# A four-layer graph attention stack: the next batch's first norm emitted inside the last layer of the batch in front, with the ends of the program rearranged

## The chip, the cores and the metric

The kernel runs on one core of one Trainium2 chip. The metric is the device time of one execution in microseconds (us); lower is better. The engines are named as in the profile: PE is the matmul engine, PEld its weight load, DVE the vector engine, ACT the scalar engine, POOL is GpSimd, and SP issues most of the DMA transfers.

## The reference, cut to what matters

The input is `x`, 32 batches of 512 nodes with 256 features, and one 512 x 512 matrix `adj` for all batches. Four graph attention layers follow each other; every one adds its result to `x`, and every one starts with a norm over the features:

```python
h = jnp.maximum(_layernorm(x, axis=-1), 0.0)
x = x + _L0_gnn_ref(h, adj, L0_gnn_W, L0_gnn_a)   # mask adj, elu
h = jnp.maximum(_layernorm(x, axis=-1), 0.0)
x = x + _L1_gnn_ref(h, adj, L1_gnn_W, L1_gnn_a)   # mask adj, relu
h = jnp.maximum(_layernorm(x, axis=-1), 0.0)
x = x + _L2_gnn_ref(h, adj, L2_gnn_W, L2_gnn_a)   # four heads of 64, mask adj, elu
h = jnp.maximum(_layernorm(x, axis=-1), 0.0)
x = x + _L3_gnn_ref(h, adj, ...)                  # two attentions between two dense layers
```

In layers 0 to 2 the attention between nodes i and j is the softmax over j of `leaky_relu(s_i + s_j)`, where `s_i` and `s_j` are the products of node i's and node j's values with the two halves of a vector `a`, and only the pairs that `adj` allows count. Layer 3 is

```python
out = relu(x @ mlp1_w + mlp1_b);          residual = out
out = elu(gat(out, None, W_fc, a_fc)) + residual       # no mask, 512 features
out = relu(out @ mlp2_w + mlp2_b);        residual = out
out = elu(gat(out, adj, W_hand, a_hand)) + residual    # mask adj
return relu(out)
```

The kernel has a fast form, which holds for some kinds of input only, and a general form, which is there for all others. A flag that the fast form computes tells whether its result may be used. All that follows is about the fast form.

## The kernel before, in words

**Tiling.** A batch's 512 nodes are four tiles of 128 rows; its `x` is one SBUF tile, 128 x (4 x 256), which all four layers update in place. A layer takes the norm of the rows on DVE and ACT (`norm`: statistics at L268 and L269, the inverse deviation with a logarithm and an exponential at L271 and L272, the scaled rows `xn` at L275 or L279), transposes `xn` on PE (`turn_pair`, recorded at L70, with `hT` written by ACT at L289), multiplies by the layer's weights (`values`, PE at L66; its results `v` are written at L318 and L319 in layer 0 and at L321, L323 and L324 in layer 1), forms the unnormalised attention weights (`weights`, L352, on DVE), and multiplies these with `v` on PE (`averages`; a column of ones gives the row sums, of which L386 takes the reciprocal). `note` keeps the largest exponential for the flag.

**Two kinds of norm.** With `late=True` (L275) only the mean is subtracted, and the scale `rs` is applied after the product. With `late=False` (L279) DVE waits for the inverse deviation and applies both. The first norm of a batch and the norm at the end of layer 2, whose rows layer 3 takes, are of this second kind.

**Streams.** Stream i (0 to 3) works on the batches i, i+4, i+8 and so on; `NS` is 4. Each stream is a Python generator that emits instructions and then yields the time at which it would like to go on (`after_us(n)`, from a count of its own PE cycles and a pause). The loop at the end of `fast` always continues the stream with the smallest time. This makes an order of emission in which the four streams, at different layers, are interleaved; a scheduler then arranges the instructions within each engine, apart from the few that `keep_in_program_order` ties. Each stream owns two of the eight PSUM banks.

`batch(b)` is one batch of a stream. It takes the `x` that was loaded earlier, makes the first norm, and runs the layers:

```python
        xn, rs = new_xn(), small([NT], "rs")
        for t0 in range(0, NT, 2):
            norm(xt, xn, rs, t0, False)
        yield after_us(4)
```

The load of batch b+4 is issued after layer 2 of batch b. All streams share three buffers for `xn`.

**Layer 3.** The attention without mask has no need of a full 512 x 512 matrix: the nodes are sorted by one of the two sums (`sort_attend`: POOL scatters the rows at L606, running sums go to a table in DRAM, POOL gathers one row per node at L654, and DVE combines its halves at L669). Only the last batch uses the full matrix (`attend`). After the dense layer `mlp2` (its result is `rT`) comes the masked attention, and the last loop of `layer3` finishes the batch by two pairs of tiles: exponential and Relu on ACT (L698, L699), a minimum, an exponential and a sum (`elu2_plus1`, L409 to L411), the residual, transposed from `rT` (L709), the last Relu (L710), the addition to `x` on POOL (L712) and the store of 256 KB (L713).

**Start.** SP issues the loads in the order of the text: x of batch 0, W0, the two halves of a0, `adj`, x of batches 1 to 3, and the other weights. `finish_w` multiplies each weight matrix with its vector `a` (`scale_a` at L110 and L111, `project` at L120 and L126), which gives three more columns. The generator `setup`, emitted between the streams, turns `adj` into the transposed mask (L209, L210, L219), then prepares the later layers' weights, and then checks `adj` for negative entries with one reduction over all of it (`differ`, L225). The reduction keeps its place in the emitted order. At the end of the program (L774 to L783) the numbers kept by `note` and `differ` are reduced to the flag.

Of the kernel before, what the change touches and what calls it, by code (L numbers as in the profile page):

```python
# [24 lines left out]
OP = mybir.AluOpType  # L25
AX = mybir.AxisListType

EPS = 1.0e-5
P = 128
# [6 lines left out]
def fast(ctx, tc, flag, x, adj, w0, a0, w1, a1, w2, a2, mlp1_w, mlp1_b, mlp2_w, mlp2_b,  # L36
         w_fc, a_fc, w_hand, a_hand, out):
    nc = tc.nc
    B, N, F = x.shape
    NT = N // P  # L40
# [5 lines left out]
    NS = 4  # L46
# [13 lines left out]
    def after_us(us):  # L60

        return begun[0] + STRETCH * spent[0] / CYCLES + SLOW * us
# [5 lines left out]
    def transpose(p, x, i, tied=False):  # L68
        spent[0] += 2 * P
        instruction = nc.tensor.transpose(p, x, i)  # L70
        if tied:
            tc.keep_in_program_order(instruction)
# [4 lines left out]
    def bank():  # L77

        own = [turn[0], *(i for i in range(NS) if i not in active and i != turn[0])]
        banks[0] += 1  # L80
        return psum.tile([P, N], FP, tag=f"b{own[banks[0] % len(own)]}", name="b", bufs=8 // NS)
# [11 lines left out]
    def load_x(b):  # L93
        t = work.tile([P, NT, F], FP, tag="x", name="x", bufs=NS + 1)
        nc.sync.dma_start(t, x[b].rearrange("(t p) f -> p t f", p=P))
        return t


    def fetch_a(a, name):
        ft = a.shape[0] // (2 * P)  # L100
        t = const.tile([P, ft, 3], FP, name=name)
        for s, c in ((0, 2), (1, 0)):
            nc.sync.dma_start(
                t[:, :, c:c + 1],
                a[s * ft * P:(s + 1) * ft * P, :].rearrange("(t p) o -> p t o", p=P),
            )
        return t

    def scale_a(t, alpha):
        nc.vector.tensor_scalar_mul(t[:, :, 1:2], t[:, :, 0:1], alpha - 1.0)  # L110
        nc.vector.tensor_scalar_mul(t[:, :, 2:3], t[:, :, 2:3], 1.0 - alpha)  # L111

    def project(dst, block, k, a_cols):

# [13 lines left out]
    def fetch_w(w, a, name):  # L128

        kt, cols = w.shape[0] // P, w.shape[1]  # L130
        t = const.tile([P, kt, cols + 3], FP, name=name)
        wr = w.rearrange("(k p) f -> p k f", p=P)
        for c in range(0, cols, F):
            nc.sync.dma_start(t[:, :, c + (3 if c else 0):c + (3 if c else 0) + F], wr[:, :, c:c + F])
        return t, fetch_a(a, name + "a")

    def finish_w(fetched, alpha):
        t, a_cols = fetched

        def block(k, f):  # L140
            c = f * P + (3 if f * P >= F else 0)
            return t[:, k, c:c + P]

        scale_a(a_cols, alpha)
        for k in range(t.shape[1]):
            project(t[:, k, F:F + 3], block, k, a_cols)
            yield


    xts = {0: load_x(0)}  # L150
    W0, _ = fetched0 = fetch_w(w0, a0, "W0")
    adj_sb = work.tile([P, NT, N], I32, tag="w", name="adj", bufs=4)
    nc.sync.dma_start(adj_sb, adj.rearrange("(t p) j -> p t j", p=P))
    for b in range(1, NS):
# [1 line left out]
    W1, _ = fetched1 = fetch_w(w1, a1, "W1")  # L156
# [6 lines left out]
    for h in range(NH):  # L163
        t, r = divmod(h * D, P)
# [8 lines left out]
    WFC, _ = fetched3 = fetch_w(w_fc, a_fc, "WFC")  # L173
    WM2 = const.tile([P, KH, F], FP, name="WM2")
    nc.sync.dma_start(WM2, mlp2_w.rearrange("(k p) f -> p k f", p=P))
    WHA, _ = fetched4 = fetch_w(w_hand, a_hand, "WHA")
# [23 lines left out]
    differ = const.tile([P, 2], FP, name="differ")  # L200
# [5 lines left out]
    def setup():  # L206

        own = work.tile([P, NT, N], FP, tag="w", name="own", bufs=4)
        nc.vector.tensor_scalar(own, adj_sb, 0.0, None, op0=OP.is_gt)  # L209
        nc.gpsimd.affine_select(  # L210
            out=own, in_=own, pattern=[[P, NT], [-1, N]], base=0, channel_multiplier=1,
            compare_op=OP.not_equal, fill=1.0,
        )
        for j in range(NT):
            turn[0] = NS - 1 - j % (NS - 1)
            p = bank()
            for t in range(NT):
                transpose(p[:, t * P:(t + 1) * P], own[:, t, j * P:(j + 1) * P], ident, j + t == 0)
            nc.scalar.copy(maskT[:, j, :], p)  # L219
        turn[0] = NS - 1  # L220
        yield
        yield from finish_w(fetched1, 0.01)


        tc.keep_in_program_order(nc.vector.tensor_reduce(differ[:, 0:1], adj_sb, AX.XY, OP.min))  # L225
        nc.vector.tensor_scalar(differ[:, 0:1], differ[:, 0:1], 0.0, None, op0=OP.is_lt)
        least = small([1], "rden")
        nc.vector.tensor_reduce(least, diag, AX.X, OP.min)
        nc.vector.tensor_scalar(differ[:, 1:2], least, 0.0, None, op0=OP.is_le)
        nc.vector.tensor_copy(W2[:, :, :, :D], raw2.rearrange("p k (h d) -> p k h d", d=D))  # L230
        nc.vector.tensor_scalar_mul(A2v[:, :, 1:2], A2v[:, :, 0:1], -0.8)
        nc.vector.tensor_scalar_mul(A2v[:, :, 2:3], A2v[:, :, 2:3], 0.8)
        for k in range(KF):
            project(W2[:, k, :, D:], lambda k, f: raw2[:, k, f * P:(f + 1) * P], k, A2)
            yield
        yield from finish_w(fetched3, 0.2)

        for tri, sign in ((before, 1), (after, -1)):
            nc.vector.memset(tri, 1.0)
            nc.gpsimd.affine_select(  # L240
                out=tri, in_=tri, pattern=[[sign, P]], base=0, channel_multiplier=-sign,
                compare_op=OP.is_gt, fill=0.0,
            )
        ties = work.tile([P, 2 * N - P], FP, tag="w", name="ties", bufs=4)
        nc.vector.memset(ties, TINY)
        nc.gpsimd.affine_select(
            out=ties, in_=ties, pattern=[[-1, 2 * N - P]], base=N - P, channel_multiplier=1,
            compare_op=OP.is_gt, fill=0.0,
        )
        nc.vector.tensor_copy(band, ties)  # L250
        yield
        yield from finish_w(fetched4, 0.2)
# [3 lines left out]
    def small(shape, name):  # L256
        return work.tile([P] + shape, FP, tag=name, name=name, bufs=2 * NS)
# [33 lines left out]
    def turned(xn, when):  # L291

        hT = work.tile([P, KF, N], FP, tag="hT", name="hT", bufs=3)
        turn_pair(xn, hT, 0)
        yield when
        turn_pair(xn, hT, 2)
        yield after_us(0.6)
        return hT
# [78 lines left out]
    def pair(tag="y"):  # L377
        return work.tile([P, 2, F], FP, tag=tag, name=tag, bufs=3)
# [10 lines left out]
    def plain(hT, w, rs=None):  # L389
        v = yield from values(hT, w, rs)  # L390
        wt = weights(lambda t: v[:, t, F + 2:F + 3], lambda j: v[:, j, F + 1:F + 2])
        note(v[:, :, F:])
        yield after_us(3.2)
        return v, wt
# [294 lines left out]
    def layer3(xt, xn, when, b):  # L689
        oT = yield from linear_t((yield from turned(xn, when)), WM1, b1, "oT", 2)  # L690
        yield from (attend if b >= B - 1 else sort_attend)(oT, b)
        rT = yield from linear_t(oT, WM2, b2, "rT", 2)
        v, wt = yield from plain(rT, WHA)
        for t0 in range(0, NT, 2):
            y, q = pair(), pair("q")
            for i in range(2):
                p, rd = averages(v, wt, t0 + i)
                nc.scalar.activation(q[:, i, :], p, AF.Exp, scale=rd)  # L698
                nc.scalar.activation(y[:, i, :], p, AF.Relu, scale=rd)  # L699
                yield after_us(0)  # L700
            elu2_plus1(y, q)
            p = bank()
            for i in range(2):
                for k in range(KF):
                    transpose(
                        p[:, (i * KF + k) * P:(i * KF + k + 1) * P], rT[:, k, (t0 + i) * P:(t0 + i + 1) * P], ident
                    )
            yf = y.rearrange("p a f -> p (a f)")
            nc.vector.scalar_tensor_tensor(yf, p, -1.0, yf, op0=OP.add, op1=OP.add)  # L709
            nc.scalar.activation(y, y, AF.Relu)  # L710
            xr = xt[:, t0:t0 + 2, :]
            nc.gpsimd.tensor_tensor(xr, xr, y, op=OP.add)  # L712
            nc.sync.dma_start(  # L713
                out[b, t0 * P:(t0 + 2) * P, :].rearrange("(t p) f -> p t f", p=P), xr
            )
            yield after_us(0)

    def mlp_in(oT, y, t):
# [7 lines left out]
            o, p.rearrange("p (f c) -> p f c", c=P), -1.0, o, op0=OP.add, op1=OP.add  # L726
        )

    def batch(b):
        xt = xts.pop(b)  # L730
        xn, rs = new_xn(), small([NT], "rs")
        for t0 in range(0, NT, 2):
            norm(xt, xn, rs, t0, False)
        yield after_us(4)
        when = after_us(2)
        for layer in (layer0, layer1, layer2):
            xn, rs, when = yield from layer(xt, xn, rs, when)
        if b + NS < B:
            xts[b + NS] = load_x(b + NS)
        yield from layer3(xt, xn, when, b)  # L740
# [13 lines left out]
    while ready:  # L754
        i = min(ready, key=ready.get)
# [23 lines left out]
    p = bank()  # L779
# [437 lines left out]
```

## The time and the profile before

| | |
|---|---|
| median of 3 runs | 2943.76 us (2943.12 to 2945.2) |
| profiled execution, its own time | 2945.59 us |
| span of that execution in the profile | 2943.9 us |
| mean granted clock of PE | 0.995 of full speed |
| busy share: PE, PEld, DVE, ACT, POOL | 97%, 79%, 76%, 52%, 17% |
| DMA, mean over the span | 92 GB/s |

The span runs from the first to the last thing that the profiler recorded; the execution's own time is 1.7 us longer. A busy share is an average over the whole span, in which the start, the long middle and the end lie together. PE and PEld overlap, so their times are not added. In lines of groups, waits and timeline a value is named as the program names it: `xn<-x,mv,rs` writes `xn` from `x`, `mv` and `rs`. `L66` and `L70` are the lines of the helpers that record every matmul and every transpose, so that they hold the work of all layers, and the operands tell these apart. In a timeline a line is a run of equal instructions: its start, the time from its first start to its last end, the engine, what it does, how many (`x4`), and in brackets how long the engine had been idle in front of it and what it waited for.

### The profile page before, as it was taken

To read this page: it belongs to the slowest core of one execution; us is meant where nothing else is said; L and a number is where in the kernel's file an instruction comes from. 1 tells how busy PE (TensorE), PEld (TensorE's weight loads), DVE (VectorE), ACT (ScalarE), POOL (GpSimd) and SP (SyncE) were. 2 spreads that over 40 slices of the span, in tenths; PEclk is the share of its full clock that TensorE was granted. 3 is DMA by queue.
4 is the path that set the end of the run, shared out by engine and by line. 5 is a ranking of instruction groups with operands and counts; after the bars stand their busy time and mean duration, and the time that the engine had idled before them with its cause. 6 is when DMAs were issued, how large, how long until landed. Compare 5 with 4: busy or idle time off the path is not lost.

```text
span 2943.9 us, 43065 instructions
## 1 busy us (share of the span) xinstructions
PE 2863.2 (97%) x15177; PEld 2326.1 (79%) x15177; DVE 2224.0 (76%) x5674; ACT 1537.4 (52%) x3918; POOL 501.3 (17%) x509
## 2 busy tenths in 40 slices
PE   7999999999999999999999999999999999999988
PEld 6777888877887877888878888778888788887766
DVE  4677877778877778878777878777777788787764
ACT  4444455554555554555554555545555555555544
POOL 0011112111122111122021121121221111221120
PEclk9999999999999999999999999999999999999999
DMA  3033223233223233233332232332232322332230
GB/s 94 19 101 99 87 83 116 92 96 99 90 87 105 95 98 98 83 102 98 98 101 90 86 107 93 96 99 89 87 116 89 99 95 81 101 112 77 96 106 23
DMA packets 193150, 270.89 MB, mean 92 GB/s; under 512 B 16992, under 2 KB 156062, under 8 KB 192928
## 3 DMA queue, kind: packets, MB, share of 16 engines
q1 hardware_dynamic: 163168, 169.76, 18.5%
q0 software_dynamic: 29760, 98.30, 10.1%
q8 instruction: 123, 2.02, 0.3%
q14 instruction: 99, 0.81, 0.1%
HBM read 152.62 MB, written 115.39 MB: 91 GB/s over the span
## 4 chain that ended last, share of the span: by engine, by line
PE 77%; DVE 13%; ACT 5%; DMA 3%; issue 1%; POOL 0%; SPq 0%; POOLq 0%; ACTq 0%; DVEq 0%
PE b L66 70%; PE b L70 7%; DVE st L268 3%; DVE xn L279 1%; DMA order<-v,at 1%; DVE xn L275 1%; DVE sums L640 1%; DVE w L352 1%; ACT v L324 1%; DMA sums<-order 1%; DVE sums L631 1%; ACT y L504 1%; DVE x L405 1%; ACT q L503 1%; DVE y L404 1%
## 5 line engine op out<-in xcount | busy, mean ns | idle before, releaser
L66 PE MATMUL b<-v,w 128*128 128x65 f32 (+1 forms) x7232 | 1222.4, 321 | 6.8 <-DVE w L352 6.7
L66 PEld LDWEIGHTS b<-v,w 128*128 128x128 f32 x7232 | 1053.6, 192 | 167.8 <-issue 64.2
L66 PE MATMUL b<-WFC,oT 128*128 128x256 f32 (+1 forms) x2048 | 496.3, 380 | 0.0
L66 PEld LDWEIGHTS b<-WFC,oT 128*128 128x128 f32 x2048 | 373.6, 189 | 48.7
L66 PE MATMUL b<-W,hT 128*128 128x259 f32 (+1 forms) x1536 | 382.0, 387 | 9.2 <-ACT hT L289 4.4
L352 DVE SCALAR_TENSOR_TENSOR w<-b,v,maskT 128x512 f32<-128x512 f32 x512 | 369.0, 743 | 4.9 <-PE b L70 3.6
L606 POOL DMA_INDIRECT order<-v,at x248 | 284.2, 1146 | 491.2 <-DVE oT L725 152.0
L66 PEld LDWEIGHTS b<-W,hT 128*128 128x128 f32 x1536 | 283.0, 190 | 58.9 <-ACT v L324 8.9
L352 DVE SCALAR_TENSOR_TENSOR w<-spread,v,maskT 128x512 f32<-128x512 f32 x384 | 269.3, 741 | 0.0
L386 DVE RECIPROCAL rden<-b 128x1 f32<-128x1 f32 (+1 forms) x516 | 78.7, 164 | 246.5 <-PE b L66 243.2
L712 POOL TENSOR_TENSOR x<-x,y 128x512 f32<-128x512 f32 x64 | 81.3, 1270 | 1074.9 <-ACT y L710 963.8
L66 PE MATMUL b<-hT,WM 128*128 128x512 f32 x512 | 248.6, 596 | 0.7 <-ACT hT L289 0.7
L654 POOL DMA_INDIRECT g<-table,at x124 | 120.9, 975 | 724.8 <-ACT y L674 385.3
L66 PE MATMUL b<-oT,WM 128*128 128x512 f32 x512 | 230.3, 592 | 0.0
L528 ACT ACTIVATE v<-b,ends 128x256 f32<-128x256 f32 x256 | 118.6, 466 | 176.7 <-PE b L66 172.4
L268 DVE BATCH_NORM_STATS2 st<-x 128x6 f32<-128x256 f32 x512 | 192.7, 408 | 5.1 <-DMA x<-in_x_dram 2.6
L289 ACT ACTIVATE hT<-b 128x512 f32<-128x512 f32 x256 | 147.0, 590 | 83.8 <-PE b L70 83.8
L338 ACT ACTIVATE oT<-b,bias 128x512 f32<-128x512 f32 x128 | 87.7, 685 | 193.2 <-PE b L66 193.2
L411 DVE TENSOR_TENSOR y<-q,y 128x512 f32<-128x512 f32 x192 | 132.5, 690 | 67.0 <-ACT q L410 66.5
L70 PE MATMUL b<-ident,xn 128*128 128x128 f32 x1024 | 152.7, 279 | 23.5 <-DVE xn L279 20.9
L66 PEld LDWEIGHTS b<-oT,WM 128*128 128x128 f32 x512 | 97.0, 190 | 95.1 <-issue 91.8
L70 PEld LDWEIGHTS b<-ident,xn 128*128 128x128 f32 x1024 | 121.9, 143 | 60.6 <-DVE xn L279 33.8
(142 smaller groups left out, 3738.3 us busy)
## 6 DMA issues: line engine op xcount, KB each, us to landing
table<-sums SPq DMA_DIRECT2D x62, 1032.0 KB
sums<-order SPq DMA_DIRECT2D x62, 516.0 KB
spread<-row SPq DMA_DIRECT2D x96, 256.0 KB
x<-in_x_dram SPq DMA_DIRECT2D x32, 512.0 KB
out_dram<-x SPq DMA_DIRECT2D x64, 256.0 KB
sums<-order SPq DMA_DIRECT2D x62, 129.0 KB
order<-v,at POOLq DMA_INDIRECT x248
g<-table,at POOLq DMA_INDIRECT x124
```

Source lines behind the costliest of these rows:

```text
L66: nc.tensor.matmul(p, w, x, **flags)
L70: instruction = nc.tensor.transpose(p, x, i)
L268: nc.vector.bn_stats(st[:, i, :], xt[:, t0 + i, :])
L289: nc.scalar.activation(hT[:, :, t0 * P:(t0 + 2) * P], p.rearrange("p (k n) -> p k n", k=KF), AF.Relu)
L338: nc.scalar.activation(o[:, f, :], p, AF.Relu, bias=bias[:, f:f + 1])
L352: w = nc.vector.scalar_tensor_tensor(wt[:, j, :], r, t_col(j), maskT[:, j, :], op0=OP.max, op1=OP.mult)
L386: nc.vector.reciprocal(r, den)
L411: nc.vector.tensor_tensor(r, q, r, op=OP.add)
L528: nc.scalar.activation(halves[c][:, t, :F], ps[:, :F], AF.Copy, scale=ends[:, t, 0:1])
L606: nc.gpsimd.indirect_dma_start(out=orders[c], out_offset=bass.IndirectOffsetOnAxis(ap=at[:, 0, t:t + 1], axis=0), in_=halves[c][:, t, :], ...
L654: nc.gpsimd.indirect_dma_start(out=g, out_offset=None, in_=table, in_offset=bass.IndirectOffsetOnAxis(ap=at[:, 1, t:t + 1], axis=0),)
L712: nc.gpsimd.tensor_tensor(xr, xr, y, op=OP.add)
```

## The change

There are five edits; no result is computed differently.

1. The first norm of batches 4 to 31 moves. A new function `first_norm(b)` holds it. For batches 0 to 3 it is called at the start of `batch(b)` as before. For a later batch b+4 it is called in `layer3` of batch b, in the last loop, after the first pair of tiles has been emitted with its store and before the second pair. The instructions are the same.
2. `scale_a` works on POOL, not on DVE.
3. The two loads of a0 are issued ahead of x of batch 0 and of W0.
4. The reduction over `adj` (`differ`, L225 before, L215 after) and the comparison behind it are emitted ahead of the transposes of the mask, behind the mask's two elementwise steps.
5. In the last batch the last loop of `layer3` takes one tile at a time. There the addition to `x` is on DVE, and four stores of 128 KB take the place of two of 256 KB. All other batches keep pairs.

```diff
     def scale_a(t, alpha):
-        nc.vector.tensor_scalar_mul(t[:, :, 1:2], t[:, :, 0:1], alpha - 1.0)
-        nc.vector.tensor_scalar_mul(t[:, :, 2:3], t[:, :, 2:3], 1.0 - alpha)
+        nc.gpsimd.tensor_scalar_mul(t[:, :, 1:2], t[:, :, 0:1], alpha - 1.0)
+        nc.gpsimd.tensor_scalar_mul(t[:, :, 2:3], t[:, :, 2:3], 1.0 - alpha)
...
-        return t, fetch_a(a, name + "a")
+        return t, fetch_a(a, name + "a") if len(a.shape) == 2 else a
...
+    a0_sb = fetch_a(a0, "W0a")
     xts = {0: load_x(0)}
-    W0, _ = fetched0 = fetch_w(w0, a0, "W0")
+    W0, _ = fetched0 = fetch_w(w0, a0_sb, "W0")
...
             compare_op=OP.not_equal, fill=1.0,
         )
+        tc.keep_in_program_order(nc.vector.tensor_reduce(differ[:, 0:1], adj_sb, AX.XY, OP.min))
+        nc.vector.tensor_scalar(differ[:, 0:1], differ[:, 0:1], 0.0, None, op0=OP.is_lt)
         for j in range(NT):
...
-        tc.keep_in_program_order(nc.vector.tensor_reduce(differ[:, 0:1], adj_sb, AX.XY, OP.min))
-        nc.vector.tensor_scalar(differ[:, 0:1], differ[:, 0:1], 0.0, None, op0=OP.is_lt)
         least = small([1], "rden")
...
-        for t0 in range(0, NT, 2):
-            y, q = pair(), pair("q")
-            for i in range(2):
+
+        n = 1 if b == B - 1 else 2
+        for t0 in range(0, NT, n):
+            y, q = pair()[:, :n, :], pair("q")[:, :n, :]
+            for i in range(n):
...
-            nc.vector.scalar_tensor_tensor(yf, p, -1.0, yf, op0=OP.add, op1=OP.add)
+            nc.vector.scalar_tensor_tensor(yf, p[:, :n * F], -1.0, yf, op0=OP.add, op1=OP.add)
             nc.scalar.activation(y, y, AF.Relu)
-            xr = xt[:, t0:t0 + 2, :]
-            nc.gpsimd.tensor_tensor(xr, xr, y, op=OP.add)
+            xr = xt[:, t0:t0 + n, :]
+            (nc.gpsimd if n == 2 else nc.vector).tensor_tensor(xr, xr, y, op=OP.add)
             nc.sync.dma_start(
-                out[b, t0 * P:(t0 + 2) * P, :].rearrange("(t p) f -> p t f", p=P), xr
-            )
+                out[b, t0 * P:(t0 + n) * P, :].rearrange("(t p) f -> p t f", p=P), xr
+            )
+            if t0 == 0 and b + NS < B:
+                first_norm(b + NS)
             yield after_us(0)
...
+    normed = {}
+
+    def first_norm(b):
+
         xt = xts.pop(b)
         xn, rs = new_xn(), small([NT], "rs")
         for t0 in range(0, NT, 2):
             norm(xt, xn, rs, t0, False)
-        yield after_us(4)
+        normed[b] = xt, xn, rs
+
+    def batch(b):
+        if b < NS:
+            first_norm(b)
+            yield after_us(4)
+        else:
+            yield after_us(4)
+        xt, xn, rs = normed.pop(b)
         when = after_us(2)
```

More of the change, by code (lines that the diff above doesn't have):

```diff
@@ L702, in layer3 @@
             p = bank()
-            for i in range(2):
+            for i in range(n):
                 for k in range(KF):
@@ L727, in mlp_in @@
         )
-    def batch(b):
+    normed = {}
+    def first_norm(b):
         xt = xts.pop(b)
```

## The prediction, before the result was known

> **What bounds the kernel now.** I read the page first, then the stages, then who waits for whom, then the timeline where the waits are. The page's busy row:
>
> ```profile
> PE 2863.2 (97%) x15177; PEld 2326.1 (79%) x15177; DVE 2224.0 (76%) x5674; ACT 1537.4 (52%) x3918; POOL 501.3 (17%) x509
> ```
>
> The same by stretches (length; busy us of PE, PEld, DVE, ACT, POOL; granted clock, DMA share, GB/s):
>
> ```profile
> 0.00:40.00 40.00, 28.30 (x138) 22.96 (x139) 16.20 (x56) 13.56 (x34) 4.08 (x10) 0.91 0.60 172
> 40.00:200.00 160.00, 147.67 (x804) 120.47 (x803) 107.93 (x310) 67.79 (x191) 11.65 (x12) 0.99 0.14 45
> 200.00:2700.00 2500.00, 2466.42 (x13144) 2009.12 (x13143) 1947.80 (x4958) 1337.70 (x3420) 445.68 (x448) 1.00 0.30 95
> 2700.00:2944.00 244.00, 220.82 (x1096) 173.60 (x1094) 152.06 (x352) 118.38 (x276) 39.90 (x39) 0.96 0.23 75
> ```
>
> PE is busy for 98.7% of the middle stretch; in all it idles 80.7 us, of which 33.6 lie there, 24.0 before 200 us and 23.2 after 2700. A change that leaves PE's work alone can win from these alone. The waits of PE (us in total, times, longest) say whom it waits for:
>
> ```profile
> PE b L70 <- DVE xn L279: 20.9, 33, 1.7
> PE b L70 <- ACT v L324: 13.0, 29, 0.9
> ```
>
> L279 is the norm's last step, with which two norms end: a batch's first, and that of its layer 3. Following the 256 L279 instructions in order tells them apart: 18.2 of the 20.9 us stand before the first transpose of a new batch. One such place (batch 19), PE alone and then DVE alone:
>
> ```profile
> 1620.90 1.91 PE L66 MATMUL b<-WFC,oT 128*128 128x259 f32 x8
> 1622.65 0.60 PE L70 MATMUL b<-ident,xn 128*128 128x128 f32 x4
> 1623.09 3.22 PE L66 MATMUL b<-WFC,oT 128*128 128x259 f32 x14
> 1627.11 0.77 PE L70 MATMUL b<-ident,xn 128*128 128x128 f32 x4 [0.80 <-DVE xn L279]
> 1627.71 0.60 PE L66 MATMUL b<-WFC,oT 128*128 128x259 f32 x2
> ```
> ```profile
> 1618.93 0.17 DVE L386 RECIPROCAL rden<-b 128x1 f32<-128x1 f32 x1 [3.28 <-PE b L66]
> ...
> 1626.64 1.51 DVE L279 TENSOR_SCALAR xn<-x,mv,rs 128x256 f32<-128x256 f32 x4
> 1628.07 0.75 DVE L669 SCALAR_TENSOR_TENSOR g<-g,ends 128x516 f32<-128x516 f32 x1
> ```
>
> The transposes stand in PE's queue before their norm is done, while DVE had idled 3.28 us eight us earlier. The real loss is over the 0.80 shown: eight WFC passes from 1620.90 to 1622.65 make 0.22 each, so the 14 from 1623.09 would have released PE at 1626.16, and it started at 1627.11 (0.95 lost); four transposes take 0.44 in flow (1622.65 to 1623.09) and took 0.60 here (0.16 lost). Together 1.11.
>
> **The skill.** "TensorE: Matmul & The Clock Gate", section "Part 1: The HAM clock gate", says that PE falls to half rate after an idle window. It does so here: the granted clock is 0.50 from 26 to 32 us after a 2.73 us wait, and the passes come every 0.43 us. "SBUF — State Buffer", section "SBUF: two separate sides", says that VectorE and GpSimd lock a shared port pair for a whole instruction; the last L409 below took 1.23 us beside POOL's L712, against a mean of 0.43. "DMA: Bandwidth & Descriptors", section "Rules for kernel authors", says that a strided last dimension costs a descriptor for each element; W0a's two loads (1 KB each) were issued from 1.86 us, and the second still held DVE until 8.32, while x's 512 KB took 3.6.
>
> **The change, part by part.**
>
> *First norm, batches 4 to 31.* Per batch 4 L268 (0.41), 4 L269 (0.17), 4 L279 (0.41) and 4 small ACT steps move; no DMA and no PE instruction does. In the two built programs, the last L279 stands one to two PE instructions before its first transpose now and some 25 to 35 instructions earlier after the change, and the transposes stand two or three matmuls earlier. DVE has the idle 3.28 us there, and x has long landed (batch 19's load was issued at 1537.9). Passed on DVE: two L386 of the batch in front, about 1.6 us later; their bank is next needed by the transposes at 1620.46, over 2 us after. On POOL and SP the out store and gathers keep their order. Over a period of four batches the PE wait is 0.43, 0.28, 0.80, 0.80 and the start-to-start loss, worked as above, 0.74, 0.50, 1.12, 1.12: 3.48, seven times: **-24.4**. Late next: in each fourth batch the first product with w (L352 starts 1329.42, 0.75) stands before v's transposes (1329.95): 0.25 more, seven times, **+1.8**. The L324 waits stay.
>
> *Head.* The order of these four decides:
>
> ```profile
> 23.41 0.32 PE L70 MATMUL b<-ident,v 128*128 128x128 f32 x1
> 23.47 2.28 DVE L225 TENSOR_REDUCE differ<-adj 128x1 f32<-128x2048 int32 x1
> 25.66 2.72 DVE L352 SCALAR_TENSOR_TENSOR w<-b,v,maskT 128x512 f32<-128x512 f32 x4
> 26.46 2.94 PE L66 MATMUL b<-v,w 128*128 128x257 f32 x6 [2.73 <-DVE w L352]
> ```
>
> The check's reduce (2.28) leaves this place for one behind `own`, where DVE idles from 12.35 to 16.35 and POOL and PE work on the mask: hidden. L352 can start at 23.9 instead of 25.66: -1.8. Against it, two loads of a0 (0.49 each on SP) go ahead of x and W0, so these start 0.98 later; adj is issued at 2.88 as before but queues behind them, and the chain of waits has adj's landing in it ("2.88 8.08 DMA adj"). Bounds 0 to +1.0, I take +0.5. The half clock after the wait: some eleven passes at 0.43 for 0.22, 2.3; with about 1 us of wait left it stays or goes, I take -1.2. The eight scalings (0.17 on DVE) go to POOL, which idles 10 us; nearest POOL row, L575's 128x8 copy, 0.19. Sum **-2.5**, ends -6 and +1.5 (another fall of the clock, as at 77 us, included).
>
> *Tail.* The last pair of tiles:
>
> ```profile
> 2932.89 1.23 DVE L409 TENSOR_SCALAR q<-q 128x512 f32<-128x512 f32 x1 [0.17 <-ACT q L698]
> ...
> 2936.49 0.63 ACT L710 ACTIVATE y<-y 128x512 f32<-128x512 f32 x1 [1.61 <-DVE y L709]
> 2937.20 1.26 POOL L712 TENSOR_TENSOR x<-x,y 128x512 f32<-128x512 f32 x1 [3.36 <-ACT y L710]
> ```
>
> The last store is issued at 2938.49 and the span ends 5.4 later. One tile at a time: L386 at 2931.9; q 0.47; the flag's reduce and compare (0.28, 0.13) until 2932.85; minimum about 0.25; exponential 0.47; the third tile's two additions and then its own two at 0.42 each (L496's row), to 2934.7; Relu 0.47; x on DVE 0.42, not on POOL for 1.26. The store is issued at about 2935.6, 2.8 earlier, and is half as large. **-3.0**, ends -1 and -4.5. Two more stores and ten more small instructions lie beside PE's products.
>
> Sum: -24.4 + 1.8 - 2.5 - 3.0 = **-28.1**. The profiled execution took 2945.59 (span 2943.9, 1.7 around it), 1.8 over the median 2943.76; from the median, 2915.7.
>
> **The rivals.**
>
> *Half of it.* What PE no longer waits for DVE it waits for somewhere else: v's L324 (13.0 in total) comes due sooner, or L715 on POOL (1.27) locks out the moved L280, so that an L386 and its bank come late. For it: DVE is at 78% in the middle, and L275 took up to 1.44 beside L712. Against it: the slack of 2 us, and L324 is local to its own stream. Only some 12 of 22.6 are won, and little at the ends: 2930.
>
> *Slower: the combine in front.* L669 (L670 after) moves on DVE from behind the norm to before the second pair's L275 of layer 1, about 4.7 us earlier. If its gather has not landed, DVE stops, and those xn, transposed next, are late on PE. Now the first gathers land 4.1 to 6.8 us after issue and, from the second batch to the one before the last few, 6.2 to 8.7 before the combine; 1.5 to 4 would remain. Each us of stop costs 28 us; from 1.0 us per batch it eats all the gain. A stop of 1.5 gives 2943.8 - 28 + 42 = 2958.
>
> *More at both ends.* The clock does not fall in the head and the tail gives its 4.5: 2908.
>
> *No change.* The norm keeps its old place: the two programs' orders say otherwise.
>
> **How the numbers follow.** As worked (2908 to 2924) 0.68; half of it (2924 to 2938) 0.18; more 0.06; no change 0.04; slower 0.04. 0.2% (5.9 us) is about what a measurement of this kernel can tell from no change: faster 0.92, same 0.04, slower 0.04. I predict 2916. The range, 2906 to 2928, takes in the ends of head (8 wide) and tail (3.5) and the upper part of "half"; about 0.18 is outside.
>
> **What would show it.** Right: the wait of PE's L70 for xn falls from 20.9 to about 5, all of it in batches 0 to 3 and the last layer 3; the middle's busy share rises from 98.7 to about 99.4%, and four batches take 353.4 us where they took 356.6; L353's wait in the head falls from 2.73 to about 1; the last store leaves 5.4 us before an end some 28 us earlier. Wrong: a wait of DVE for g of over 0.5 us a batch (it is 14.4 in all now), a new PE wait for L387 or an L70 for v over 1.2, or the head's first product later than 26.5.

## The result, and the profile after

The kernel after takes 2934.64 us (median of 10 runs, 2927.16 to 2941.32), the kernel before, timed beside it, 2944.32 (10 runs, 2941.33 to 2946.87). The ratio is 0.9966 with a 95% interval of 0.9957 to 0.9975: faster by 9.7 us, where 28.1 were forecast. The measured time lies outside the stated range, 2906 to 2928. The profiled execution of after took 2931.35 (span 2929.6). I follow the losses in it.

The page's busy row and the middle stretch, to be held against those of before:

```profile
PE 2858.9 (98%) x15177; PEld 2329.5 (80%) x15177; DVE 2219.9 (76%) x5676; ACT 1536.8 (52%) x3922; POOL 502.3 (17%) x515
```
```profile
200.00:2700.00 2500.00, 2468.07 (x13175) 2018.14 (x13174) 1947.08 (x4967) 1341.11 (x3431) 449.75 (x451) 1.00 0.30 96
```

PE is busy for 98.7% of the middle, as before; 99.4% was forecast. The waits of PE say that something was won and something else came in:

```profile
PE b L66 <- DVE v L463: 14.1, 7, 2.9
PE b L66 <- DVE w L353: 10.5, 18, 0.9
PE b L70 <- ACT v L325: 9.2, 22, 0.9
...
PE b L70 <- DVE xn L280: 4.0, 5, 1.9
```

The wait for the norm (L279 before, L280 now) fell from 20.9 to 4.0, as forecast. The first line had no counterpart before: seven waits, one in every fourth batch, 1.1 to 2.9 us each, for the second step of layer 2's values (L462 before, L463 now). One of the seven, beside batch 19, on PE and then on DVE:

```profile
1889.89 2.84 PE L66 MATMUL b<-W,hT 128*128 128x268 f32 x12
1895.65 2.95 PE L66 MATMUL b<-W,hT 128*128 128x268 f32 x12 [2.92 <-DVE v L463]
```
```profile
1888.97 0.69 DVE L412 TENSOR_TENSOR y<-q,y 128x512 f32<-128x512 f32 x1 [1.77 <-ACT ends L528]
1890.51 0.17 DVE L306 TENSOR_REDUCE seen<-ends 128x1 f32<-128x12 f32 x1 [0.84 <-ACT ends L528]
1894.44 0.76 DVE L670 SCALAR_TENSOR_TENSOR g<-g,ends 128x516 f32<-128x516 f32 x1 [3.77 <-DMA g<-table,at]
1895.12 0.87 DVE L463 SCALAR_TENSOR_TENSOR v<-b,rs,v 128x256 f32<-128x256 f32 x2
```

DVE stands for 3.77 us at a combine (L670) that waits for its gather, and two L463 stand behind it. They need nothing of that gather: they belong to another stream. That ACT and DVE take their queue strictly in order is what the Trainium skill says ("TensorE: Matmul & The Clock Gate", "Part 1: The HAM clock gate", under the array's details). This trace agrees: the first two `v` were ready for DVE when ACT's lines end, at 1891.26 and 1893.04, and DVE, idle meanwhile, began them at 1895.12, right behind the combine:

```profile
1890.99 0.27 ACT L462 ACTIVATE v<-b,rs 128x12 f32<-128x12 f32 x1
...
1892.77 0.27 ACT L462 ACTIVATE v<-b,rs 128x12 f32<-128x12 f32 x1 [0.23 <-PE b L66]
```

Until they have read their banks PE cannot write more products with `W2`. Which of a batch's four combines this is the view does not say, since it leaves buffer numbers out. The built programs do, and the trace agrees: the combine that stops waits for the gather that its batch issued third. This is DVE's order at that place, in words (`v2` is one L463, or L462 before; tiles are counted from 1):

```
before   v2, v2, combine of tile 3, v2, v2, combine of tile 2
after    combine of tile 3, v2, v2, v2, v2, combine of tile 2
```

The gathered rows have two buffers, so the third tile's gather is issued only when the first tile's buffer is free. On POOL and SP:

```profile
1887.68 0.95 POOL L655 DMA_INDIRECT g<-table,at  x1 [2.19 <-ACT y L675]
```
```profile
1885.53 0.40 SPq L716 DMA_DIRECT2D out_dram<-x  x1
1887.73 0.38 SPq L95 DMA_DIRECT2D x<-in_x_dram  x1
```

It landed 6.30 us after its issue, at 1893.98, and the combine began 0.46 later. In the kernel before the same seven gathers (batches 3, 7, ... 27) took 4.2 to 4.7 us, since the x load had been issued 3.3 to 4.0 us ahead of them and the store 6.2 us ahead; now the load goes out within 0.6 us of the gather and the store 2.2 us ahead.

### The profile page after: what moved, and what is told of

Same layout as the page of the kernel before. It is cut to its first block, busy times and chain, and to the rows that moved or that the text cites. A ratio compares the mean times of both kernels' runs of the same rounds, so it can differ in the third digit from the quotient of the medians.

```text
span 2929.6 us, 43083 instructions
## 1 busy us (share of the span) xinstructions
PE 2858.9 (98%) x15177; PEld 2329.5 (80%) x15177; DVE 2219.9 (76%) x5676; ACT 1536.8 (52%) x3922; POOL 502.3 (17%) x515
## 4 chain that ended last, share of the span: by engine, by line
PE 82%; DVE 10%; ACT 4%; DMA 3%; issue 1%; SPq 0%; POOL 0%; DVEq 0%; POOLq 0%; ACTq 0%
PE b L66 75%; PE b L70 7%; DVE st L269 2%; DMA g<-table,at 2%; DVE sums L641 1%; DVE xn L280 1%; DVE x L406 1%; DVE y L405 1%; ACT v L325 1%; DVE sums L632 1%; ACT y L505 1%; ACT q L504 1%; DVE w L353 1%; ACT hT L290 1%; DVE tot L646 0%
## 5 line engine op out<-in xcount | busy, mean ns | idle before, releaser
L66 PE MATMUL b<-v,w 128*128 128x65 f32 (+1 forms) x7232 | 1218.0, 321 | 10.6 <-DVE w L353 10.5
L66 PEld LDWEIGHTS b<-v,w 128*128 128x128 f32 x7232 | 1050.0, 191 | 168.7 <-issue 56.1
L66 PE MATMUL b<-WFC,oT 128*128 128x256 f32 (+1 forms) x2048 | 495.2, 380 | 0.0
L66 PEld LDWEIGHTS b<-WFC,oT 128*128 128x128 f32 x2048 | 374.5, 189 | 49.3
L66 PE MATMUL b<-W,hT 128*128 128x259 f32 (+1 forms) x1536 | 388.8, 391 | 22.8 <-DVE v L463 14.1
L607 POOL DMA_INDIRECT order<-v,at x248 | 277.0, 1117 | 490.7 <-DVE oT L730 152.3
L66 PEld LDWEIGHTS b<-W,hT 128*128 128x128 f32 x1536 | 285.3, 192 | 75.3 <-DVE v L463 17.1
L715 POOL TENSOR_TENSOR x<-x,y 128x512 f32<-128x512 f32 x62 | 87.8, 1416 | 1063.7 <-ACT y L713 950.0
L66 PE MATMUL b<-hT,WM 128*128 128x512 f32 x512 | 250.0, 599 | 0.7 <-ACT hT L290 0.7
L66 PE MATMUL b<-oT,WM 128*128 128x512 f32 x512 | 231.2, 594 | 0.0
L387 DVE RECIPROCAL rden<-b 128x1 f32<-128x1 f32 (+1 forms) x516 | 77.3, 162 | 184.8 <-PE b L66 183.0
L412 DVE TENSOR_TENSOR y<-q,y 128x512 f32<-128x512 f32 (+1 forms) x194 | 132.9, 685 | 82.9 <-ACT q L411 45.0
L66 PEld LDWEIGHTS b<-oT,WM 128*128 128x128 f32 x512 | 97.5, 191 | 95.7 <-issue 92.4
```

What stands on the lines that cost most here:

```text
L66: nc.tensor.matmul(p, w, x, **flags)
L387: nc.vector.reciprocal(r, den)
L412: nc.vector.tensor_tensor(r, q, r, op=OP.add)
L607: nc.gpsimd.indirect_dma_start(out=orders[c], out_offset=bass.IndirectOffsetOnAxis(ap=at[:, 0, t:t + 1], axis=0), in_=halves[c][:, t, :], ...
L715: (nc.gpsimd if n == 2 else nc.vector).tensor_tensor(xr, xr, y, op=OP.add)
```

## The experiments

Three theories. **A**: DVE's queue. The move makes the third combine float ahead of all four L463 in every fourth batch, and its gather, not landed, holds PE through them. **B**: ACT. L463 waits for ACT's L462 (90 us in DVE's waits, 56 before), and the moved norm's small ACT steps make that late. **C**: the clock. The new start sets off falls of PE's clock that take the gain back.

All kernels were timed in several rounds beside the kernel before (medians 2944.1 to 2945.0 in the four groups of runs). Times are medians, with the ratio to before and its 95% interval.

**1. The combines tied to each other.** `keep_in_program_order` puts an instruction behind whatever its engine was given just before, here a `note` of another stream that itself is early. One edge more:

```diff
-            tc.keep_in_program_order(
+            combined.append(tc.keep_in_program_order(
                 nc.vector.scalar_tensor_tensor(z, z, ends[:, t, 2:3], g[:, 2 * C:], op0=OP.mult, op1=OP.add)
-            )
+            ))
+            if t:
+                behind(combined[t], combined[t - 1])      # an edge of order on DVE, no semaphore
```

> The kernel after, with one thing more: the combine of each gathered tile is also kept behind the combine of the tile in front of it on DVE. This moves, in seven batches (7, 11, ... 31 less the last), the third tile's combine (L670) from in front of the four L463 of another stream to behind them; nothing else changes place. Theory A (in these batches DVE stops at the third combine for its gather, and the L463 queued behind it hold PE): the seven PE waits for L463, 14.1 us in the profile after and 15.3 from start to start, go, and with them the clock falls behind the longest of them, some 2 to 5 us: 2934.6 - 17 to 20 = about 2916, and the runs lie within 5 us of each other. Rival B (L463 is late because ACT's L462 is, as the waits of DVE say with 90 us, ACT being pushed by the moved norm): the order of the combine changes nothing, 2934 and the wait for L463 stays near 14. Rival C (falls of PE's clock that the new head sets off): 2934, with granted clocks again between 0.992 and 0.997.

Measured: **2916.57** (2913.41 to 2918.26), ratio 0.9901 [0.9888, 0.9914]: 18.1 below after. (The seven batches are 3, 7, ... 27; the text on record counts them wrongly.) No L463 appears among PE's waits. The same place in this kernel, DVE and PE:

```profile
1885.03 0.48 DVE L469 SCALAR_TENSOR_TENSOR v<-b,rs,v 128x256 f32<-128x256 f32 x1 [0.62 <-ACT v L468]
1886.81 0.49 DVE L469 SCALAR_TENSOR_TENSOR v<-b,rs,v 128x256 f32<-128x256 f32 x1 [1.29 <-ACT v L468]
1887.71 0.48 DVE L469 SCALAR_TENSOR_TENSOR v<-b,rs,v 128x256 f32<-128x256 f32 x1 [0.41 <-ACT v L468]
1889.49 0.48 DVE L469 SCALAR_TENSOR_TENSOR v<-b,rs,v 128x256 f32<-128x256 f32 x1 [1.29 <-ACT v L468]
1889.89 0.75 DVE L676 SCALAR_TENSOR_TENSOR g<-g,ends 128x516 f32<-128x516 f32 x1
1890.55 0.20 DVE L312 TENSOR_REDUCE seen<-v 128x1 f32<-128x48 f32 x1
1890.67 0.16 DVE L393 RECIPROCAL rden<-g 128x1 f32<-128x1 f32 x1
1890.75 0.74 DVE L676 SCALAR_TENSOR_TENSOR g<-g,ends 128x516 f32<-128x516 f32 x1
```
```profile
1883.62 5.53 PE L66 MATMUL b<-W,hT 128*128 128x268 f32 x24
```

The four L469 (L463 of after) come first, each as soon as ACT's L468 is done; PE makes its 24 products without a stop; and the combine waits for nothing, though the third tile's gather still took 6.62 us (it is the second L676 here). In the two traces PE, ACT, POOL and SP have the same instructions in the same order, and on DVE only these seven combines stand elsewhere. B falls: ACT did not hold L463. The middle:

```profile
200.00:2700.00 2500.00, 2481.88 (x13279) 2032.62 (x13278) 1965.13 (x4999) 1350.84 (x3457) 453.23 (x454) 1.00 0.30 96
```

PE is busy for 99.3% of it, and four batches take 353.5 to 353.9 us.

**2. The norm's move alone**, on the kernel before (edit 1; the other four left out).

> The kernel before, with the move of the first norm alone (edit 1; start and end as before). Theory A: the 22.6 of the forecast's steady part less 15 to 20 for the third combine: 2944.3 - 5 = about 2939 (2936 to 2943), with PE waits of 10 to 16 us for L462 (the same line as L463 of after). Rival B gives the same time, with the same waits, but for another reason. Rival C (the ends cost it): the full 22.6 is there, 2922.

Measured: 2942.69 (2937.22 to 2946.25), ratio 0.9996 [0.9988, 1.0004]. The main edit alone gains nothing that is measurable; A's 2939 was some 4 too low, its range just held. The wait is there:

```profile
PE b L66 <- DVE v L462: 14.3, 7, 2.9
```

**3. The other four edits alone** (the first norm back at its batch's start).

> The kernel after, with the first norm back at the start of its batch (edits 2 to 5 alone). Theory A and rival B: the ends give 3.0 at the tail and between 0 and 2.5 at the head, 2940 (2938 to 2942), L463 holds PE nowhere. Rival C: the new head brings clock falls, 2944 or more, with clocks spread between 0.992 and 0.997.

Measured: 2937.55 (2932.57 to 2949.11, 22 runs), ratio 0.9978 [0.9971, 0.9985]. C falls: the ends gain 7 us, more than I had given them, though these runs spread over 16.5 us.

**4. The norm's move with the tie**, start and end as before.

> The kernel before, with the move of the first norm and the tie of the combines, start and end as before. Theory A: the steady part of the forecast in full, 2944.3 - 22.6 = 2922 (2919 to 2925). Rival B: as with the norm alone, about 2939. Rival C: 2922.

Measured: 2923.71 (2919.31 to 2924.48), ratio 0.9922 [0.9909, 0.9935]. This is theory A's full gain. With kernel 2 it isolates the tie (19 us), with kernel 1 the ends (7.1 again).

**5. The tie alone**, on the kernel before.

> The kernel before with the tie of the combines alone (no other edit). In the profile before, the same seven third combines already stand in front of two of the four L462 and stop DVE for 1.0 to 1.4 us, but no PE wait for L462 shows. Theory A: the order costs nothing as long as the stop is short and two L462 are in front of it; same time as before, 2944 within 2. A rival, that the tie brings something of its own in any kernel (some 18 us, as it does on top of after): 2927.

Measured: 2947.08 (2941.1 to 2951.71), ratio 1.0006 [0.9997, 1.0014]: no gain, and no loss clear of noise. The traces show that the tie moved the same seven combines here and nothing else. In the kernel before, two of the four `v2` stood in front of the third combine, which freed both banks of their stream, so that DVE's stop of 0.9 to 1.4 us passed beside products that PE could go on with. The same place in the kernel before, DVE and PE:

```profile
1901.03 0.49 DVE L462 SCALAR_TENSOR_TENSOR v<-b,rs,v 128x256 f32<-128x256 f32 x1 [0.38 <-ACT v L461]
1902.35 0.48 DVE L462 SCALAR_TENSOR_TENSOR v<-b,rs,v 128x256 f32<-128x256 f32 x1 [0.83 <-ACT v L461]
1903.97 0.75 DVE L669 SCALAR_TENSOR_TENSOR g<-g,ends 128x516 f32<-128x516 f32 x1 [1.14 <-DMA g<-table,at]
1904.64 0.87 DVE L462 SCALAR_TENSOR_TENSOR v<-b,rs,v 128x256 f32<-128x256 f32 x2
```
```profile
1899.16 5.53 PE L66 MATMUL b<-W,hT 128*128 128x268 f32 x24
```

**6, 7, 8. The ends, one edit undone at a time in the tied kernel.** The check's reduce back at its old place (6); the last batch in pairs (7); a0's loads behind W0 and the scaling on DVE (8).

```diff
 6  -  tc.keep_in_program_order(nc.vector.tensor_reduce(differ[:, 0:1], ...))  # ahead of the mask's transposes
    +  tc.keep_in_program_order(nc.vector.tensor_reduce(differ[:, 0:1], ...))  # behind finish_w(fetched1)
 7  -  n = 1 if b == B - 1 else 2
    +  n = 2
 8  -  a0_sb = fetch_a(a0, "W0a")            # and nc.gpsimd in scale_a
    +  fetch_w(w0, a0, "W0")                 # and nc.vector in scale_a
```

> The kernel after with the tie, with the check's reduce back at its old place (edit 4 undone). The first four weights of batch 0 wait again for 2.28 us of DVE: the forecast's head gives 1.8 for it and 1.2 for a shorter clock fall: 2916.6 + 3 = 2919.5. If the clock falls that stand at 40 and 75 us in the profile of after and of the tied kernel take the gain back: 2916.6 within 1.

> The kernel after with the tie, with the last batch finished in pairs of tiles again (edit 5 undone). The forecast's tail: 2916.6 + 3.0 = 2919.5 (2917.5 to 2921).

> The kernel after with the tie, with the loads of a0 behind W0 and the scaling on DVE as before (edits 2 and 3 undone). In the forecast these two cost 0.5 or less; from the difference of the two ends measured so far (7 us, of which the tail has some 3 and the reduce some 3) they gain about 1: 2916 to 2918. PE starts about 1.2 earlier (5.3 for 6.5), and the third product of the start is not earlier.

Measured, against 2916.57: (6) 2919.69 (2915.72 to 2921.94), 3.1 more, close to the forecast; but these are five runs each, their ranges and the intervals of their ratios overlap, so the median alone does not show it. (7) 2917.3 (2915.86 to 2925.4, four runs), 0.7 more, just below the range on record, which alone would not tell the edit from nothing; in the profiles the stretch from the 15,130th matmul to the end is 21.3 with pairs and 18.0 with single tiles, 3.3 shorter. (8) 2915.67 (2913.22 to 2917.21, four runs), 0.9 less, within the error: no gain of these two edits shows. The first product of the start with the weights `w`, in the tied kernel and then in kernel 8:

```profile
25.23 2.87 PE L66 MATMUL b<-v,w 128*128 128x257 f32 x12 [0.84 <-DVE w L359]
```
```profile
23.14 2.87 PE L66 MATMUL b<-v,w 128*128 128x257 f32 x12 [0.84 <-DVE w L358]
```

The two small loads in front make W0 come 1.2 us later (PE starts at 6.51 for 5.33), and the first product 2.1 later. The medians are too close to say how much of this reaches the end.

**9. The x load emitted later**, on after, to take it away from the third gather.

```diff
-        if b + NS < B:
-            xts[b + NS] = load_x(b + NS)      # in batch(), behind layer 2
+        if b + NS < B:
+            xts[b + NS] = load_x(b + NS)      # in layer3(), in front of linear_t(oT, WM2, ...)
         rT = yield from linear_t(oT, WM2, b2, "rT", 2)
```

> The kernel after (no tie), with the load of the next x (512 KB) issued later in layer 3, after the second attention's table has been read, not after layer 2. In the profile after this load is issued within 0.1 us of the third gather of batches 7, 11, ... 27, and that gather takes 5.55 us (median) where it took 4.30 before. The order on DVE stays. Theory A says that PE's wait follows the landing of that gather one to one: landing 1 to 1.5 us earlier, seven times, takes 7 to 10 us off: 2934.6 - 9 = 2926, PE's wait for L463 6 to 8 us where it was 14.1. A rival (only the place in the queue counts, as DVE and PE are out of step whenever L463 stands behind the combine): 2934, waits unchanged.

Measured: 2935.29, ratio 0.9968 [0.996, 0.9977], L463 waits 14.7. This looks like the rival, but the load had not moved: in the trace SP's order is that of after, and the load still went out 0.05 to 0.16 us behind the gather. The experiment did not make its difference; its profile serves as a second sample of the wait.

**12. The same load, kept in SP's order** (`keep_in_program_order` on its DMA, no tie of the combines).

> The kernel after (no tie), with the load of the next x emitted in layer 3 in front of the second dense layer and kept there in SP's order. In the run before, the later emission alone had left the load where it was: it waits for the store that frees its buffer, and goes out within 0.15 us of the third gather either way. Now it comes some 140 matmuls behind that gather. The order on DVE stays. In the profiles of after, of the norm alone and of the later load, each PE wait for L463 in batches 7 to 27 is the gather's time less 3.7 us (5.01 gives 1.28, 5.54 gives 1.81, 6.29 gives 2.56, and 6.42 gives 2.69). Theory A with the collision: the gather takes 4.3 to 4.7 as in the kernel before, each wait is 0.6 to 1.0, seven of them 4 to 7 where they were 14.1; time 2934.6 - 9 = 2926 (2922 to 2929). If the load has no part in it (the store 2.2 us ahead of the gather does it, or the gather is longer for another reason): gather 5 to 6.5, wait 14, 2935.

Measured: **2927.55** (2923.67 to 2930.34), ratio 0.9941 [0.9927, 0.9955]. The load now goes out 37 to 41 us behind the gather, the seven gathers take 4.3 to 5.3 us, and the waits are less than half in sum:

```profile
PE b L66 <- DVE v L465: 6.4, 7, 1.5
```

Issue to landing, and PE's wait behind it, of the seven gathers (from the traces):

| batch | 3 | 7 | 11 | 15 | 19 | 23 | 27 |
|---|---|---|---|---|---|---|---|
| after: gather / wait | 4.87 / 1.14 | 5.01 / 1.28 | 5.54 / 1.81 | 5.55 / 1.82 | 6.30 / 2.92 | 6.29 / 2.56 | 6.33 / 2.60 |
| kernel 12: gather / wait | 4.63 / 0.89 | 4.39 / 0.65 | 4.31 / 0.57 | 4.46 / 0.73 | 4.61 / 0.87 | 4.86 / 1.12 | 5.28 / 1.54 |

The wait is the gather's time less 3.73 or 3.74 us in every place but one (batch 19 of after, where the combine began 0.36 later than elsewhere). So the waits have two factors: the place in DVE's queue, without which there are none (kernel 1, where these gathers took up to 7.7 us), and the x load beside the gather, which makes some 55% of their sum (a fifth of it in batch 3, two thirds and more in batches 11 and 19). The store still goes out 2.2 us ahead of the gather in kernel 12, so it alone does not make the gathers as long as they are in after.

The time is less clear than the waits. From the 1900th to the 14,150th matmul kernel 12 took 2321.9 us in its profile, and after 2325.8 with a fall of the clock in it. That is 3.9 less, where the waits for this `v` alone fell by 7.7. Other waits of PE came in (those of L66 for L327 went from 3.0 to 4.3 us between 400 and 2620 us, those for L278 from none to 0.9), and what the rest is stays open. So the 7.1 us between the medians of the two kernels agree with the expectation, but cannot be put down to the gather alone.

**10, 11. A step further.** In the tied kernel the middle has 2.3 us of PE waits left in four batches; some are for layer 1's `v`, behind a product of 128 x 1 on DVE. That product on ACT (10) and on POOL (11):

```diff
-                nc.vector.tensor_tensor(both, rs[:, t:t + 1], pj, op=OP.mult)
+10              nc.scalar.activation(both, pj, AF.Copy, scale=rs[:, t:t + 1])
+11              nc.gpsimd.tensor_tensor(both, rs[:, t:t + 1], pj, op=OP.mult)
```

> The kernel after with the tie, and the product of rs and the exponential in layer 1 (both, 0.15 us on DVE) made on ACT, where its input and its reader are. What is left to PE in the middle is 2.3 us of waits in four batches, nearly all of them for L331, which waits for that product behind DVE's queue, and for L359. If ACT takes it without delay: 2916.6 - 7 x 2 = 2903 to 2910. If ACT's 128 more instructions or the new order of the scheduler bring waits of their own: 2917 to 2925.

> The same product on POOL. POOL is idle for 83% of the span, but its additions of x (1.3 us) and its gathers and scatters (1.0 to 1.1 us each) stand in front of it in places: 2908 to 2920, and PE waits for L331 of over 1 us where a scatter is in front.

Measured: 2917.81 (2915.93 to 2920.13) and 2920.95 (2920.94 to 2926.93). Neither gains, and 11 lies just above its range: the wait for layer 1's `v` all but goes, and PE waits for L359, the masked weights, instead. PE's waits in kernel 10:

```profile
PE b L66 <- DVE w L359: 22.4, 41, 1.4
```

It had been 10.2 in the tied kernel. The best versions are the tied kernel and the same with the old loads (1 and 8), 28 to 29 us below before.

## Why the prediction was wrong, by its own steps

**First norm, -24.4, and +1.8 late next: right, but for a term that was left out.** From the 1900th to the 14,150th matmul the kernel before took 2331.4 us, after 2325.8, the tied kernel 2309.2. The tied kernel gains 22.2 in this stretch of six and a half periods of four batches, where the sum had 22.6 for seven; its period is 353.5 to 353.9 where 353.4 was forecast. The +1.8 is there too, in another form than stated: between 382 and 2700 us PE waits 4.8 us for L359 of the tied kernel (L352 before), where the kernel before has no such wait, and 11.0 for L331 (L324) where it had 14.4, which makes 1.4 more. "The L324 waits stay" was wrong. After kept only 5.6 of the 22.2.

**The step that failed** is the list of what is passed and what is late next. It followed the norm, its transposes and the first combine, and asked whether that combine's gather would have landed. I had counted 1.5 to 4 us of slack there, and the medians are 1.8 to 4.2, so that rival rightly did not come. I did not ask it of the third combine, whose gather is issued only after the first combine is done and has the least slack of the four (the fourth's lands 10 us ahead of its combine): before, DVE already stopped for it by 0.9 to 1.4 us in the same seven batches. That stop lay in DVE's 14.4 us of waits for `g`, which the prediction named only as a sign to watch. The sign came: these waits are 26.2 us in after, 0.8 a batch where 0.5 was to show that it is wrong. What to compute was 7 x (gather's time - 3.73), and with the gathers' times of before even this gives 4.5 us, not 15. The rest comes from the second thing missed: "On POOL and SP the out store and gathers keep their order" was true of the order and said nothing of the time. The gather went from 3.3 to 4 us behind the x load to right beside it.

So the result is the **slower** rival's mechanism, a combine in front whose gather has not landed, in another tile, with other work behind it, and in seven batches in place of 28. Measured from the start of one matmul to the start of the next, against the tied kernel, it cost 15.3 us in the seven places, and 1.5 more behind a fall of the clock. The **half of it** rival had the time (2924 to 2938) and the wrong reason: the waits for L325 went down from 13.0 to 9.2, and no PE wait for L387 shows. **No change** was ruled out rightly.

**Head, -2.5.** The ends together are worth 7.1, measured twice; the tail's profile has 3.3 of it, which leaves some 4 for the head. That is a remainder, not a measurement: in the profiles the first 1900 matmuls took 381.8 us before and 381.2 after. The reduce's move gives 3.1 in the medians (forecast 1.8 + 1.2), not clear of noise; in the profiles kernel 6 is 3.8 us behind the tied kernel at the 1900th matmul. a0's loads cost 0.9 in the medians, within the error (forecast +0.5, bounds 0 to +1.0), though the start's first product with `w` came 2.1 later with them. (The head's ends, -6 and +1.5, lie 7.5 apart, not 8.) In after the reduce stands where it was expected, and the wait for the first weights fell to 0.84 (forecast about 1):

```profile
12.33 2.28 DVE L215 TENSOR_REDUCE differ<-adj 128x1 f32<-128x2048 int32 x1
14.64 0.15 DVE L216 TENSOR_SCALAR differ<-differ 128x1 f32<-128x1 f32 x1
```

The half clock from 26 to 32 us is gone, but one came at 41 to 52 us and took the lead back in this execution: PE was 3.8 us ahead of the kernel before at 39 us, and 0.05 at 52.6.

**Tail, -3.0.** 3.3 in the profiles (kernel 7 against the tied kernel). The last store is issued 5.4 us before the end with pairs and 4.4 with single tiles, so some 1.0 of it comes with the smaller store and 2.3 with the earlier issue, where the sum had 0.2 and 2.8, and the sign "5.4 us before an end" did not come. The rest of the mechanism is as worked: the halved L410 takes 0.27 to 0.29 (1.23 for the whole one before, beside POOL), and the addition to x 0.41 to 0.43 on DVE (1.26 on POOL):

```profile
2922.30 0.29 DVE L410 TENSOR_SCALAR q<-q 128x256 f32<-128x256 f32 x1
...
2924.92 0.42 DVE L715 TENSOR_TENSOR x<-x,y 128x256 f32<-128x256 f32 x1 [0.15 <-ACT y L713]
```

## What to carry to other kernels

When instructions are moved into an engine's idle time, list all the waits on that engine which the idle time used to cover, above all those for transfers that start last, and not only the waits beside the moved work; a wait that costs nothing today is a price as soon as something unrelated stands behind it. An edge that keeps an instruction behind "the one emitted before it" holds nothing if that one can itself move: tie it to what it should really follow. If a change loses the time that it should gain, find the one wait that is new by name; here the tie that removed it took 18 us off.

## What the runs showed of the hardware that was not expected

In the seven batches the third gather (128 rows of 4 KB) took 4.2 to 4.7 us in the kernel before, where a 512 KB load had been issued 3.3 to 4.0 us ahead of it, and 4.9 to 6.3 us in after, where that load went out within 0.6 us (5.0 to 7.1 in kernel 9). Where the load came 37 us or more behind it, in kernel 12, it took 4.3 to 5.3. The load is not all: in batch 12 of the kernel before the third gather took 5.6 us with the load 3.3 us ahead.

In the middle stretch, PE's clock fell only behind waits of over 2.5 us, and not behind all of them: five of the nine such waits in the profiles of after, kernel 2 and kernel 9, and none of the twelve of 1.1 to 1.9 us. The one in after, PE and then the stretch around it:

```profile
2251.95 4.56 PE L66 MATMUL b<-W,hT 128*128 128x268 f32 x12 [2.56 <-DVE v L463]
```
```profile
2250.00:2260.00 10.00, 8.05 (x33) 6.72 (x34) 4.21 (x11) 2.96 (x7) 0.17 (x1) 0.83 0.00 0
```

The same twelve products took 2.95 us at 1895.65, where the wait was longer and the clock stayed. Outside the middle stretch the clock also fell without such a wait: the fall at 41 us in after has no wait over 0.47 us in the 15 us ahead of it. The Trainium skill ("TensorE: Matmul & The Clock Gate", "Part 1: The HAM clock gate") gives a free-running window of about 3.4 us that has to pass idle. The traces agree with such a step: every fall in the fourteen profiles, the last of each (in the tail) left out, lasted 3.41 us or two, three or five times that. That chance decides agrees with a window that runs freely; that waits of 2.6 to 2.9 us were enough, with PE busy on both sides, is less than it says. The ten runs of after spread over 14 us with mean clocks from 0.992 to 0.997, the five of the tied kernel over 5, and 35 runs of before over 11. That the falls make this spread is likely from the clocks, but no run isolates it.
